# Four segments for five in the choice among equal numbers of a top-p row, and one scan for a scan and a subtraction

## The chip, the cores and the metric

The kernel runs on one core of one Trainium2 chip. The metric is the device time of one execution in microseconds (us). Its engines work side by side, each through its own queue in order: TensorE (PE; PEld is its weight load), VectorE (DVE), ScalarE (ACT), GpSimd (POOL), and SyncE (SP), which here only issues DMAs. They wait for one another through semaphores.

## The reference, cut to what matters

Two graph layers over 2,708 nodes with 256 features. The first multiplies a sparse weighted adjacency matrix by the features, projects the result, adds the input and normalizes. The second runs two steps, each with an attention of top-p kind over all nodes; the change lies in the second of these.

```python
def _top_p_attention(X, W1, W2, W3):
    q = X @ W1.T @ W2.T
    k = X @ W3.T
    probs = jax.nn.softmax(q @ k.T / TAU, axis=-1)
    idx = jnp.argsort(-probs, axis=-1)
    sp = jnp.take_along_axis(probs, idx, axis=-1)
    cs = jnp.cumsum(sp, axis=-1)
    keep_sorted = cs - sp < TOP_P
    mask = jnp.zeros(probs.shape, dtype=bool).at[rows, idx].set(keep_sorted)
    A = probs * mask
    return A / jnp.maximum(A.sum(-1, keepdims=True), 1e-12)
...
for n in range(STEPS):
    A = _top_p_attention(Xa, W1, W2, W3)
    Xf = R @ Xf
    Xa = A @ Xa
    Z = Z + Xf @ U1[n].T + Xa @ U2[n].T
h = X + Z
...
```

In words: of each row, the largest probabilities are kept until their sum reaches 0.9. The number at which that happens is the threshold of the row. Several entries may equal it exactly, and then only the first few of them, in the order of the columns, are kept.

## The kernel before

The rows are cut into 22 blocks of 128 (the last has 20). `fast_path` holds everything that runs on ordinary data; if any of a set of flags is raised on the way, `general_path` computes the second layer anew at the end, which takes far longer.

Stages in time: the adjacency product of layer 0 (to about 290 us), step 1 of the attention (to about 760), step 2 (766 to 1323), a short end with the last normalizations (to 1343.5). No planner orders the work: the order of each engine's queue is the order in which the Python code emits the instructions.

Step 2 is the loop `for per in range(NB + 1)` at L1127. One turn, a period, works on four blocks at once. ACT and PE prepare the exponentials of block `per + 2` (`logits`, `exps2`). ACT tries two levels of the search on block `per + 1` (`try_act`, L921 and L924). DVE finishes block `per` (`last_level`, then `finish2`). PE turns the finished block `per - 1` (L525), ACT copies the turned pieces out of PSUM (L528), and PE multiplies them (L562). The product with R runs beside it in units (`r_units`, L729), fed by gathers that POOL issues (L697). From period 13 on the final normalizations join (`final_slot`, L1036 on DVE, L1046 on ACT, L1061 and L1062 on POOL). Each period has six slots `g`. `finish2` is a generator: it gives up its turn at each `yield`, and the next slot resumes it. In slot 4 it goes from the first sums (L988) through the first three replacements of L1006; after the `yield` there, DVE takes what ends a unit of R (L752, or L767 with a row block of `za` that a DMA has brought), and slot 5 resumes with the rest.

A row is held in 2,720 columns: 2,708 and 12 of padding. What `finish2` does with a block:

- L975: of all entries, take those below an upper level into `w`, and sum them.
- L978: the eight largest of each of 20 pieces of 136 columns, so 160 candidates (`cand`).
- `put_in_order` (L575, L577): the 48 largest of the candidates, in order.
- L988 to L993: running sums, the threshold `th`, and `nk`, how many entries equal to it are to be kept.
- L997: a 1 at each candidate that equals the threshold. L998: how many of them lie in each of `WS` = 5 segments of the row (544 columns each, 32 candidates), in `num`.
- L999: the running sum of these numbers. L1000: number + `nk` - running sum, which is how many equal entries are left to keep at the start of each segment (`run`).
- L1001, L1003: for each segment eight numbers, the threshold as often as entries are to be kept there, else 0 (`part`).
- L1006: for each segment, a copy of the exponentials into `w` in which the first entries equal to the numbers of `part` are replaced by a huge number. Each is two instructions, a load of the eight numbers and the pass over the segment.
- L1009: keep what is above the threshold, and sum it; this releases PE's turning of the block.

A segment that holds eight or more equal entries raises a flag at the end (L1204, L1205).

Of the kernel before, what the change touches and what calls it, by code (L numbers as in the profile page):

```python
# [12 lines left out]
ALU = mybir.AluOpType  # L13
AX = mybir.AxisListType
# [11 lines left out]
NS2 = 20  # L26
TOP1 = 64
TOP2 = 48
WS = 5

# [20 lines left out]
def gnn_two_layer_kernel(ctx: ExitStack, tc: tile.TileContext, N, xT_d, x_d, adj_d, w0_d, b0_d,  # L53
# [71 lines left out]
    with fast:  # L125
        fast_path(fast, tc, c, flags, fint, xT_d, x_d, w0_d, b0_d, w1_d, w2_d, w3_d, u1_d, u2_d, g_d, b_d)
# [22 lines left out]
def fast_path(ctx, tc, c, flags, fint, xT_d, x_d, w0_d, b0_d, w1_d, w2_d, w3_d, u1_d, u2_d, g_d, b_d):  # L149
    nc = tc.nc  # L150
    N, D, DA, NB, DC, KH, CHS, rows = c.N, c.D, c.DA, c.NB, c.DC, c.KH, c.CHS, c.rows
# [234 lines left out]
    for t in range(NB):  # L386
        p = rows(t)
# [57 lines left out]
    for m in range(NB):  # L445
        p = rows(m)
# [123 lines left out]
    def put_in_order(dst, n, cand, p):  # L570

        spare = small.tile([P, NS2 * 8], FP, tag="spare", name="spare", bufs=1)[:, :cand.shape[1]]
        src = cand
        for i in range(0, n, 8):
            nc.vector.max(dst[:p, i:i + 8], src[:p])  # L575
            if i + 8 < n:
                nc.vector.match_replace(spare[:p], dst[:p, i:i + 8], src[:p], -3.0e38)  # L577
                src = spare
# [36 lines left out]
    def finish1(t):  # L615
# [4 lines left out]
        s = srt[:p, :TOP1]  # L620
        sc = small.tile([P, 3 + 2 * WS], FP, tag="sc", name="sc", bufs=3)
        top, mass, tot, fm = (sc[:p, i:i + 1] for i in range(4))
# [158 lines left out]
    def e2(t):  # L781
        return es[(t + 2) % 4]
# [11 lines left out]

    bulk = small.tile([P, 5 + WS, NB], FP, tag="bulk", name="bulk", bufs=1)
    nc.gpsimd.memset(bulk[:, :4, :], 1.0)
# [116 lines left out]
    w = tile1[:, :NW]  # L913
# [52 lines left out]
    def finish2(b):  # L966

        t, p = b.t, b.p
        sc = small.tile([P, 3 + 2 * WS], FP, tag="sc", name="sc", bufs=3)
        num, run = bulk[:p, 5:, t], sc[:p, :WS]  # L970
        need, below, mass, tot = (bulk[:p, i, t:t + 1] for i in range(1, 5))
        nk = sc[:p, WS:WS + 1]
        th = b.m
        e = e2(t)[:p]
        nc.vector.scalar_tensor_tensor(w[:p], e, b.d, e, op0=ALU.is_lt, op1=ALU.mult, accum_out=below)  # L975
        cand = small.tile([P, NS2 * 8], FP, tag="cand", name="cand", bufs=2)
        for i in range(NS2):
            nc.vector.max(cand[:p, 8 * i:8 * i + 8], w[:p, SEG2 * i:SEG2 * (i + 1)])  # L978
            if i in (2, NS2 // 2 + 1):
                yield  # L980
        yield
        srt = small.tile([P, TOP1 + 1], FP, tag="srt", name="srt", bufs=3)
        s = srt[:p, :TOP2]
        put_in_order(srt, TOP2, cand, p)
        yield
        x = sums
        q_ = small.tile([P, TOP1], FP, tag="qs", name="qs", bufs=1)[:p, :TOP2]
        nc.vector.scalar_tensor_tensor(need, b.z, TOP_P - 1.0, below, op0=ALU.mult, op1=ALU.add)  # L988
        nc.vector.tensor_tensor_scan(x[:p, 1:TOP2 + 1], s, s, 0.0, op0=ALU.add, op1=ALU.bypass)
        nc.vector.scalar_tensor_tensor(q_, x[:p, 1:TOP2 + 1], need, s, op0=ALU.is_ge, op1=ALU.mult)  # L990
        nc.vector.tensor_reduce(th, q_, AX.X, ALU.max)
        nc.vector.scalar_tensor_tensor(q_, x[:p, :TOP2], need, s, op0=ALU.is_lt, op1=ALU.mult, accum_out=mass)
        nc.vector.tensor_scalar(q_, q_, th, None, op0=ALU.is_equal, op1=ALU.add, accum_out=nk)  # L993

        eq = small.tile([P, NS2 * 8], FP, tag="spare", name="eq", bufs=1)
        part = small.tile([P, WS, 8], FP, tag="part", name="part", bufs=1)
        nc.vector.tensor_scalar(eq[:p], cand[:p], th, None, op0=ALU.is_equal)  # L997
        nc.vector.tensor_reduce(num, eq[:p].rearrange("p (s k) -> p s k", s=WS), AX.X, ALU.add)  # L998
        nc.vector.tensor_tensor_scan(run, num, num, 0.0, op0=ALU.add, op1=ALU.bypass)  # L999
        nc.vector.scalar_tensor_tensor(run, num, nk, run, op0=ALU.add, op1=ALU.subtract)  # L1000
        nc.vector.tensor_tensor(part[:p], run[:, :, None].to_broadcast([p, WS, 8]),  # L1001
                                ranks[:p, None, :].to_broadcast([p, WS, 8]), op=ALU.is_gt)
        nc.vector.tensor_scalar(part[:p], part[:p], th, None, op0=ALU.mult)  # L1003
        W = NW // WS
        for i in range(WS):
            nc.vector.match_replace(w[:p, W * i:W * (i + 1)], part[:p, i, :], e[:, W * i:W * (i + 1)], 3.0e38)  # L1006
            if i == WS // 2:
                yield
        nc.vector.scalar_tensor_tensor(e, w[:p], th, e, op0=ALU.is_gt, op1=ALU.mult, accum_out=tot)  # L1009
        ra = small.tile([P, 1], FP, tag="ra", name="ra")  # L1010
        nc.vector.reciprocal(ra[:p], tot)
        ras[t] = ra
# [114 lines left out]
    for per in range(NB + 1):  # L1127
# [12 lines left out]
        for g in range(NG):  # L1140
# [28 lines left out]
            if g == 0:  # L1169
                if b_dve:  # L1170
                    last_level(b_dve)
                    masks = finish2(b_dve)
                    next(masks)
                final_slot(0)
                if per > 1:

                    t = t_mul - 1
                    base = za_load(t)
                    later[0].append(lambda t=t, base=base: arrive(t, base, accs.pop(t), ras.pop(t)[:rows(t)]))
            elif masks:  # L1180
                next(masks, None)
                if b_exp and g == 5:
                    begin_search(b_exp)
# [4 lines left out]
    t = EDGE  # L1188
# [3 lines left out]
    for f in later[0] + later[1]:  # L1192
# [8 lines left out]
    nc.vector.tensor_tensor(kept, kept, bulk[:, 0, :], op=ALU.add)  # L1201
    nc.vector.scalar_tensor_tensor(flags[:, 4 * NB:5 * NB], kept, 1.0 + TIE_EPS, bulk[:, 4, :],
                                   op0=ALU.mult, op1=ALU.is_lt)
    nc.vector.tensor_reduce(flags[:, 5 * NB:6 * NB], bulk[:, 5:, :].rearrange("p w t -> p t w"), AX.X, ALU.max)  # L1204
    nc.vector.tensor_scalar(flags[:, 5 * NB:6 * NB], flags[:, 5 * NB:6 * NB], 8.0, None, op0=ALU.is_ge)  # L1205
    nc.vector.tensor_reduce(fcol, flags, AX.X, ALU.add)
    pf = ps_misc()
    nc.tensor.matmul(pf[:1, :1], lhsT=fcol, rhs=onec, start=True, stop=True)
# [386 lines left out]
```

## Time and profile before

| what | value |
|---|---|
| three timed runs | 1348.48, 1345.78 and 1349.26 us; median 1348.48 |
| profiled execution | 1345.32 us, of which 1343.5 are the span of the trace |
| busy over the span | PE 1246.7 us (93%), DVE 1045.5 (78%), ACT 753.4 (56%), POOL 640.1 (48%) |
| chain that ended last, by engine | PE 54%, DVE 38%, ACT 4% |
| its largest lines of DVE | L978 6%, L1006 5%, L1009 5%, L975 4% |
| L978, 128x136, 440 instructions | 284 ns each, 93.5 us |
| L1006, the passes over 128x544, 105 instructions | 709 ns each, 73.5 us |
| mean granted TensorE clock | 0.971 of full speed |

The span is what the trace covers; the profiled execution's own time adds 1.8 us around it. The chain follows the end of the work back, at each step to what released it, or to the instruction before it on its engine. Timelines give start, duration, engine, line, operation, output and inputs with their shapes; "x2" counts instructions that were put together, and a bracket names what ended an idle time.

### The profile page before, as it was taken

Reading aid. Unit: us, or ns where it says so; the run is one execution under the profiler, and the core shown is the slowest. Engines: PE = TensorE matmul, PEld = TensorE weight load, DVE = VectorE, ACT = ScalarE, POOL = GpSimd, SP = SyncE. Lnnn points to the kernel's source line nnn. Section 1 sums busy time; section 2 is a strip of 40 time slices with the busy share of each in tenths; the row PEclk is TensorE's granted clock in tenths of the full one; section 3 lists DMA queues with packets and bytes.
Section 4 is the critical chain, followed back from the end, with each engine's and each line's share of the span. In section 5 each row is a group of like instructions: output and inputs, shape, how many; then the busy total and the mean of one; then the engine's idle time right before and its main releaser. Section 6 shows DMA issues by size and latency. Waiting matters only on the chain.

```text
span 1343.5 us, 18721 instructions
## 1 busy us (share of the span) xinstructions
PE 1246.7 (93%) x5676; PEld 881.0 (66%) x5676; DVE 1045.5 (78%) x3488; ACT 753.4 (56%) x1366; POOL 640.1 (48%) x591
## 2 busy tenths in 40 slices
PE   8999999989899999999999789999998998999885
PEld 6877878833467666667666367676765765666663
DVE  2544545865998888777751599999999999999997
ACT  1010001035556556655555567887878888999851
POOL 1000000004465522777654478877725757777770
PEclk9999999989899999999999889999998999999988
DMA  7455554512131210232223355554522633454341
GB/s 188 163 172 162 164 164 143 166 51 72 60 98 57 71 58 9 74 102 81 71 68 97 98 166 169 148 160 147 161 66 92 191 119 122 150 172 146 122 144 37
DMA packets 92829, 157.92 MB, mean 118 GB/s; under 512 B 16356, under 2 KB 65196, under 8 KB 92720
## 3 DMA queue, kind: packets, MB, share of 16 engines
q1 hardware_dynamic: 66434, 100.59, 23.6%
q0 software_dynamic: 20544, 51.17, 13.4%
q10 hardware_dynamic: 5742, 4.89, 1.3%
q8 instruction: 47, 0.77, 0.2%
q14 instruction: 62, 0.51, 0.1%
HBM read 125.33 MB, written 31.26 MB: 117 GB/s over the span
## 4 chain that ended last, share of the span: by engine, by line
PE 54%; DVE 38%; ACT 4%; issue 2%; POOL 1%; DMA 1%; SPq 0%; ACTq 0%; DVEq 0%; POOLq 0%
PE acc L562 16%; PE acc L255 15%; PE lg L505 6%; DVE cand L978 6%; DVE w L1006 5%; DVE e L1009 5%; DVE w L975 4%; PE tr L525 4%; DVE srt L575 3%; DVE spare L577 3%; PE misc L676 3%; PE acc L648 2%; PE acc L460 2%; PE misc L424 2%; PE misc L390 2%
## 5 line engine op out<-in xcount | busy, mean ns | idle before, releaser
L528 ACT COPY wT<-tr 128x512 f32<-128x512 f32 (+2 forms) x258 | 131.9, 519 | 223.4 <-PE tr L525 219.0
L562 PE MATMUL acc<-ya,wT 128*128 128x256 f32 (+1 forms) x924 | 236.3, 396 | 12.1 <-ACT wT L528 11.7
L697 POOL DMA_INDIRECT yg<-yf_d,ix x154 | 194.8, 1265 | 78.7 <-PE misc L729 40.6
L697 POOL DMA_INDIRECT yg<-v_d,ix x154 | 193.8, 1259 | 79.4 <-DMA v_d<-v 34.0
L562 PE MATMUL acc<-x,wT 128*128 128x256 f32 (+1 forms) x924 | 230.5, 388 | 0.0
L562 PEld LDWEIGHTS acc<-x,wT 128*128 128x128 f32 (+1 forms) x924 | 165.2, 189 | 79.6 <-issue 46.9
L562 PEld LDWEIGHTS acc<-ya,wT 128*128 128x128 f32 (+1 forms) x924 | 172.1, 194 | 68.2 <-ACT wT L528 23.1
L255 PE MATMUL acc<-y,adj_t 128*128 128x257 f32 (+1 forms) x924 | 208.4, 381 | 0.0
L255 PEld LDWEIGHTS acc<-y,adj_t 128*128 128x128 f32 (+1 forms) x924 | 171.8, 189 | 32.7 <-issue 8.9
L365 POOL DMA_INDIRECT adj_t<-in_adj,ix x154 | 164.7, 1069 | 51.5 <-issue 39.9
L729 PE MATMUL misc<-yg,adj_t 128*128 128x256 f32 (+1 forms) x660 | 173.9, 397 | 9.4 <-DVE v L752 9.4
L505 PE MATMUL lg<-k,q 64*128 64x512 f32 (+3 forms) x528 | 150.7, 598 | 21.5 <-ACT e L821 19.5
L525 PE MATMUL tr<-ident,e 128*128 128x128 f32 (+2 forms) x946 | 149.9, 278 | 18.0 <-DVE e L1009 17.9
L729 PEld LDWEIGHTS misc<-yg,adj_t 128*128 128x128 f32 (+1 forms) x660 | 118.4, 193 | 56.1 <-issue 16.2
L525 PEld LDWEIGHTS tr<-ident,e 128*128 128x128 f32 (+2 forms) x946 | 114.0, 141 | 62.2 <-issue 23.9
L332 POOL DMA_DIRECT2D part_d<-e x1 | 0.6, 576 | 286.9 <-DVE e L331 286.9
L568 DVE MAX8 cand<-e 128x8 f32<-128x170 f32 (+1 forms) x352 | 87.3, 318 | 35.4 <-ACT e L512 35.4
L921 ACT ACTIVATE w<-e,st 128x2708 f32<-128x2708 f32 (+1 forms) x43 | 113.5, 2640 | 0.0
L437 ACT COPY x1T<-tr 128x256 f32<-128x256 f32 (+1 forms) x22 | 8.0, 364 | 186.6 <-PE tr L436 186.6
L924 ACT ACTIVATE w<-e,st 128x2708 f32<-128x2708 f32 (+1 forms) x42 | 110.9, 2641 | 0.1
L978 DVE MAX8 cand<-w 128x8 f32<-128x136 f32 (+1 forms) x440 | 93.5, 284 | 0.8
L575 DVE MAX8 srt<-spare 128x8 f32<-128x128 f32 (+3 forms) x264 | 81.3, 308 | 9.1
(228 smaller groups left out, 1761.8 us busy)
## 6 DMA issues: line engine op xcount, KB each, us to landing
adj_t<-in_adj SPq DMA_DIRECT2D x44, 704.0 KB
adj_t<-adjc_d SPq DMA_DIRECT2D x44, 448.0 KB
adjc_d<-adj_t SPq DMA_DIRECT2D x22, 256.0 KB
base<-za_d SPq DMA_DIRECT2D x41, 128.0 KB
adjc_d<-adj_t SPq DMA_DIRECT2D x22, 192.0 KB
xt<-in_x ACTq DMA_DIRECT2D x21, 128.0 KB
x_d<-x SPq DMA_DIRECT2D x21, 128.0 KB
x1b_d<-xb SPq DMA_DIRECT2D x21, 128.0 KB
```

The source lines that it names most:

```text
L255: nc.tensor.matmul(acc[:p, :n], lhsT=halves[k // KH][:kw, k % KH, :p], rhs=y[:kw, k, :n], start=k == 0, stop=stop and k == NB - 1)
L365: nc.gpsimd.indirect_dma_start(out=a[:CW, i, :], out_offset=None, in_=adj_rows, in_offset=bass.IndirectOffsetOnAxis(ap=ix[:CW, m, i:i + 1] ...
L505: nc.tensor.matmul(lg[:p, h, :b - a], lhsT=q[o, t * P:t * P + p], rhs=keys[s][o, i, :b - a], start=True, stop=True)
L525: nc.tensor.transpose(tr[:kw, k % 4, :p], e[:p, k * P:k * P + kw], ident[:p, :p])
L528: nc.scalar.copy(wT[:, :full, :p], tr[:, :full, :p])
L562: nc.tensor.matmul(acc[:p, :D], lhsT=wT[:kw, k % 4, :p], rhs=y[:kw, k, :], start=k == 0, stop=k == NB - 1)
L575: nc.vector.max(dst[:p, i:i + 8], src[:p])
L697: nc.gpsimd.indirect_dma_start(out=y[:CW, i, :], out_offset=None, in_=rows_d, in_offset=bass.IndirectOffsetOnAxis(ap=ix[:CW, m, i:i + 1], ...
L729: nc.tensor.matmul(acc[:p, :D], lhsT=a[:kw, k, :p], rhs=rhs, start=k == 0, stop=k == CC)
L921: nc.scalar.activation(scr[:b.p, :N], e, AF.Relu, bias=b.nz, scale=b.l[k], accum_out=b.relu)
L924: nc.scalar.activation(scr[:b.p, :N], e, AF.Sign, bias=b.nz, scale=b.l[k], accum_out=b.sign)
L978: nc.vector.max(cand[:p, 8 * i:8 * i + 8], w[:p, SEG2 * i:SEG2 * (i + 1)])
```

## The change

The candidates equal to the threshold are counted in four segments of 680 columns (40 candidates each) in place of five of 544. The counts are taken with a minus sign, by the reduction itself. `nk` is written into the first column of `run`, and one running sum, which starts from it and adds the negative counts of the first three segments, fills the other three: `run` holds the same numbers as before, and the addition and subtraction of L1000 is gone. `part` has 32 columns for 40, and L1006 runs four times on 680 columns. The `yield` inside that loop comes after its third turn, as before; behind it stands one turn for two. The flag compares the least of the negative counts with -8; a segment is now wider, and the bound of eight stays.

```diff
-WS = 5
+WS = 4
...
         num, run = bulk[:p, 5:, t], sc[:p, :WS]
         need, below, mass, tot = (bulk[:p, i, t:t + 1] for i in range(1, 5))
-        nk = sc[:p, WS:WS + 1]
+        nk = run[:, 0:1]
...
         nc.vector.tensor_scalar(eq[:p], cand[:p], th, None, op0=ALU.is_equal)
-        nc.vector.tensor_reduce(num, eq[:p].rearrange("p (s k) -> p s k", s=WS), AX.X, ALU.add)
-        nc.vector.tensor_tensor_scan(run, num, num, 0.0, op0=ALU.add, op1=ALU.bypass)
-        nc.vector.scalar_tensor_tensor(run, num, nk, run, op0=ALU.add, op1=ALU.subtract)
+        nc.vector.tensor_reduce(num, eq[:p].rearrange("p (s k) -> p s k", s=WS), AX.X, ALU.add, negate=True)
+        nc.vector.tensor_tensor_scan(run[:, 1:], num[:, :WS - 1], num[:, :WS - 1], nk, op0=ALU.add, op1=ALU.bypass)
...
-    nc.vector.tensor_reduce(flags[:, 5 * NB:6 * NB], bulk[:, 5:, :].rearrange("p w t -> p t w"), AX.X, ALU.max)
-    nc.vector.tensor_scalar(flags[:, 5 * NB:6 * NB], flags[:, 5 * NB:6 * NB], 8.0, None, op0=ALU.is_ge)
+    nc.vector.tensor_reduce(flags[:, 5 * NB:6 * NB], bulk[:, 5:, :].rearrange("p w t -> p t w"), AX.X, ALU.min)
+    nc.vector.tensor_scalar(flags[:, 5 * NB:6 * NB], flags[:, 5 * NB:6 * NB], -8.0, None, op0=ALU.is_le)
```

## The prediction

> **What bounds the kernel now.** I read the page first, then the chain of waits, a table of busy time by stretch of step 2, the waits by engine, and last the timelines of one period on VectorE (DVE) and TensorE (PE). The 40 slices of the page:
>
> ```profile
> PE   8999999989899999999999789999998998999885
> DVE  2544545865998888777751599999999999999997
> PEclk9999999989899999999999889999998999999988
> ```
>
> The change lies in `finish2`, which runs once for each of the 22 row blocks of step 2, from 766 us on. From there DVE stands at 9, with PE at 8 to 9 beside it, so the share of busy time does not settle which of them sets the pace. The chain of waits does, for one block:
>
> ```profile
> 936.73 3.07 DVE w L975 x2
> 940.25 2.09 DVE cand L978 x10
> 952.05 2.17 DVE w L1006 x4
> 956.04 3.07 DVE e L1009 x2
> 961.17 3.07 DVE w L975 x2
> ```
>
> From the L975 of one block to that of the next it never leaves DVE; the period is 961.17 - 936.73 = 24.44 us. DVE reports no wait of any size in these periods; its idle part is the 20 to 40 ns between neighbours. Two periods, before and after the final normalizations join:
>
> ```profile
> core 0: us, PE busy (x) PEld busy (x) DVE busy (x) ACT busy (x) POOL busy (x), PEclk, DMA share, GB/s
> 936.70:961.20 24.50, 23.24 (x113) 17.13 (x112) 23.46 (x80) 19.99 (x34) 18.52 (x15) 1.00 0.50 151
> 1138.00:1165.00 27.00, 24.14 (x113) 17.12 (x112) 25.82 (x90) 25.09 (x41) 21.46 (x19) 1.00 0.47 147
> ```
>
> ```profile
> 957.27 1.03 PE L729 MATMUL misc<-yg,adj_t 128*128 128x256 f32 x4
> 959.25 0.63 PE L525 MATMUL tr<-ident,e 128*128 128x128 f32 x4 [0.94 <-DVE e L1009]
> 1161.76 1.03 PE L729 MATMUL misc<-yg,adj_t 128*128 128x256 f32 x4
> 1162.71 0.63 PE L525 MATMUL tr<-ident,e 128*128 128x128 f32 x4
> ```
>
> In the first period PE stands idle for 0.94 us until L1009 has written the masked block: PE has that much room. In the second the transposes start 0.15 us after DVE's last write for L1009 (1162.56), the same lag as at 959.25, so DVE still paces; but the four matmuls before, which elsewhere let the next start 0.86 us after their first, would have freed PE at 1162.62. The loop of ACT and PE has 0.09 us of room there, in six periods (14 to 19 of 0 to 21; 1111 to 1272 us).
>
> **What the skill says.** "Vector Engine (DVE) Microarchitecture Reference", 5.2 "Measured stream behaviour on trn2": 1.0417 ns for a column and about 75 ns for an instruction after overlap. The trace agrees in the slope: the match-replace takes 276 ns on 128 columns and 709 on 544, that is 1.041 each. "DVE: opcode table, instruction layouts, handler registers and perf-mode slots", 6 "Datapath and trigger behaviour": the scan runs at half rate. It agrees: 170 ns for 5 columns (L999), 256 for 48 (L989), 2.0 each. "SBUF — State Buffer", section "SBUF: two separate sides": DVE and GpSimd share a port pair under an exclusive lock. Here L1003 takes 0.24 us in 17 blocks and 0.47 to 0.49 in 5, and those five begin 0.47 us after the start of a gather on POOL and end where it ends. No page gives the price of a [P, 1] scalar operand.
>
> **The change part by part.** The lines of DVE at stake, of one block (start, duration):
>
> ```profile
> 950.72 0.32 DVE L998 TENSOR_REDUCE bulk<-eq 128x5 f32<-128x160 f32 x1
> 951.07 0.17 DVE L999 TENSOR_TENSOR_SCAN sc<-bulk 128x5 f32<-128x5 f32 x1
> 951.28 0.23 DVE L1000 SCALAR_TENSOR_TENSOR sc<-bulk,sc 128x5 f32<-128x5 f32 x1
> 951.54 0.20 DVE L1001 TENSOR_TENSOR part<-sc,ranks 128x40 f32<-128x40 f32 x1
> 951.77 0.24 DVE L1003 TENSOR_SCALAR part<-part,st 128x40 f32<-128x40 f32 x1
> 952.05 0.09 DVE L1006 MATCH_VALUE_LOAD w<-part,e 128x8 f32 x1
> 952.13 0.71 DVE L1006 MATCH_REPLACE8 w<-part,e 128x544 f32<-128x544 f32 x1
> 952.76 0.08 DVE L1006 MATCH_VALUE_LOAD w<-part,e 128x8 f32 x1
> ```
>
> What counts on a full engine is the distance between starts, not the duration.
>
> 1. L999 and L1000 become one scan over 3 columns. Removed: 951.54 - 951.07 = 0.47 us. Added: L999's 170 ns less two columns at 2.0 (166), plus a start value read from a tile. The trace has no scan with such a start. Nearest rows: a tensor_scalar on one column takes 134 ns with constants (L827), 214 with one tile scalar (L942), 273 with two (L828), so 60 to 80 ns for each. I take 65: 231 ns, and with the usual 33 ns to the next start 0.265. Saved 0.205; ends 0.27 (the read is free) and 0.15 (it costs double). A loss is excluded: the scan would have to take 270 ns more than L999.
> 2. L1006 goes from five pairs over 544 columns to four over 680: the same 2,720 columns, one pair fewer. A pair lies 0.695 us from the next, of which 544 x 1.041 = 0.566 are columns, so 0.129 fixed, and that is saved. Ends 0.11 and 0.15 (the start distances of the pairs scatter from 0.69 to 0.71).
> 3. L1001 and L1003 shrink from 40 columns to 32: 8 ns each at most, 0.015 together. L998 reads the same 160 columns; its negation I cost at nothing, at most 11 ns (L592 with it 181 ns, L594 without 170, same shape).
> 4. The reduce of the flags at the end reads 88 columns for 110: 0.02 us once. One memset on POOL (L797) shrinks far ahead of its use. No DMA is added, removed or moved past another, and PE, ACT, POOL and SP keep their instructions in the same order.
> 5. Moved: the first half of L1006, ahead of the yield, still has three pairs, now 3 x 0.142 = 0.43 us longer. The L752 or L767 behind it therefore starts about 0.2 us later in its block, net of points 1 and 3. It frees a PSUM bank and lets a row of `v` or `za` be stored; the bank that L767 frees at 1158.1 is written next at 1161.8. More than 3 us of room, no cost. What follows it, one pair for two, is shorter by more.
>
> Sum for a block: 0.205 + 0.129 + 0.015 = 0.35 us (ends 0.27 and 0.43). Times 22: 7.7 us (5.9 to 9.4).
>
> **Whether it reaches the end.** In periods 0 to 13, PE's 0.94 us shrinks to some 0.6 and every 0.35 counts (in the two of them in which PE shows no wait, from 790 and from 1034 us, it makes up for it in the next). In the six tight periods ACT and PE can follow by 0.09 only; DVE gains 0.26 on them each time, 1.6 us in all. It is not stopped at once, since it does not wait for the loop at the period's start: the nearest thing it needs is a `za` row from DMA landing 2.0 us before its use (1182.69 against 1184.68), then `yg` from POOL with 3.0 (1175.15 against 1178.18), then L958 after ACT's last small step with about 4. In period 20 the exponentials are gone and PE waits 3.4 us for L1009, room for the 1.6. After the last block the chain is mostly DVE again (1322 to 1337 us), so all 22 savings arrive.
>
> Against the profiled execution, 1345.32 us (span 1343.5): 1345.32 - 7.7 = 1337.6. That execution was the fastest of four, 3.2 us below the median of the three timed ones (1348.48); their common mean is 1347.2, so I forecast 1347.2 - 7.7 = 1339.5, or -0.57%.
>
> **Rivals.**
>
> A. The loop of ACT and PE holds: DVE meets a wait once it is ahead, and in the six tight periods only 0.09 comes through. 16 x 0.35 + 6 x 0.09 = 6.1 us, 1341.1. For it: the room of 0.09. Against: the 2 to 4 us that DVE may run ahead.
>
> B. Port holds eat the gain. A small tensor_scalar that begins 0.45 to 0.85 us into a gather waits up to 0.25 us for its end. L1003 moves up by 0.2 us in its block, which at the present phases releases the five held ones (-1.2 us) and catches three others by 0.08 us each; but the gathers, 1.25 us apart, move too. If most blocks were caught at both L997 and L1003, 0.2 to 0.25 us each, the gain would fall to between 0 and 4 us: about 1345. For it: six holds are there already. Against: 16 of 22 blocks have none, and nothing aims at that window.
>
> C. Slower: PE's clock. The granted clock is 0.93 in 790 to 815 us, where PE is busy all of its 24.3 us. A denser step could draw such a grant in periods 1 to 9: (23.14 / 0.94) + 0.3 of waits = 24.9 against 24.44 now, +0.45 x 9 = 4.1; in the six tight periods about 4 us of the loop are PE, +0.25 against the 0.09, so +0.16 x 6 = 1.0; the other seven keep -0.35, -2.4. Together +2.7 us, 1350. It decides below a grant of 23.14 / (24.44 - 0.3) = 0.96. Against: most periods show 1.00 with PE at 95%.
>
> That the change makes more flags is a rival in kind: a segment may now hold the equals of 680 columns before the slow general path is entered at 8. Numbers exactly equal to a threshold are rare in a row of float exponentials; 1%, and far slower.
>
> **Chances.** Forecast 0.65, A 0.12, B 0.15, C and the flags 0.08. About 0.3%, 4.0 us, is what a measurement here tells from no change. The forecast and A are faster by more (0.77), B is within (0.15), C and the flags slower (0.08). Range: low 1347.2 - 9.4 - 2 of scatter = 1335.5; high from the upper half of B, 1345.5. What is left out is the slow side and the rest of B.
>
> **What would show it.** Right: L975 to L975 at 24.1 us before 1050; a scan of about 0.23 us; L1006 of 0.85 us four times a block; PE's wait for L1009 near 0.6 in the first periods and none in the tight ones. Wrong: a DVE wait at L767 or L1036 after 1110 (A), tensor_scalars of 0.4 to 0.5 us in most blocks (B), a granted clock below 0.96 over many periods (C), a scan above 0.4 us.

## The result, and the profile after

The changed kernel takes 1338.76 us in the median of four runs (1337.47 to 1339.33), before it was 1348.7: a ratio of 0.9929, with a 95% interval from 0.9912 to 0.9947. Run once more, the pair gave 0.9934 (0.9920 to 0.9948). The profiled execution took 1338.91 us, its span 1337.1.

The 40 slices of the page after, to be laid beside those of before:

```profile
PE   8999999979899999999999979999998998899885
DVE  2445555865998888877761399999999999999997
PEclk9999999989899999999999779999999989999987
```

They look the same, as they must: DVE is as full as before and only comes through its work sooner. The chain of waits for one block shows it (start, duration):

```profile
935.45 3.07 DVE w L975 x2
...
950.62 2.60 DVE w L1005 x5
953.22 0.39 DVE v L752
953.61 0.85 DVE w L1005
954.49 3.07 DVE e L1008 x2
...
959.61 3.05 DVE w L975
```

From L975 to L975 it is 959.61 - 935.45 = 24.16 us, where it was 24.44, and the chain still never leaves DVE. The operations at stake, from DVE's timeline of the same block:

```profile
949.45 0.32 DVE L998 TENSOR_REDUCE bulk<-eq 128x4 f32<-128x160 f32 x1
949.81 0.22 DVE L999 TENSOR_TENSOR_SCAN sc<-bulk,sc 128x3 f32<-128x3 f32 x1
950.07 0.19 DVE L1000 TENSOR_TENSOR part<-sc,ranks 128x32 f32<-128x32 f32 x1
950.29 0.29 DVE L1002 TENSOR_SCALAR part<-part,st 128x32 f32<-128x32 f32 x1
950.62 0.09 DVE L1005 MATCH_VALUE_LOAD w<-part,e 128x8 f32 x1
950.70 0.85 DVE L1005 MATCH_REPLACE8 w<-part,e 128x680 f32<-128x680 f32 x1
951.47 0.08 DVE L1005 MATCH_VALUE_LOAD w<-part,e 128x8 f32 x1
```

The scan and what follows it lie 0.26 us apart, where scan and subtraction took 0.47. L1002, with fewer columns than before, is longer (0.29 against 0.24); this comes back below. PE and the end of L1008, from their timelines:

```profile
956.00 1.03 PE L729 MATMUL misc<-yg,adj_t 128*128 128x256 f32 x4
957.69 0.63 PE L525 MATMUL tr<-ident,e 128*128 128x128 f32 x4 [0.66 <-DVE e L1008]
...
1237.60 1.03 PE L729 MATMUL misc<-yg,adj_t 128*128 128x256 f32 x4
1238.47 0.60 PE L525 MATMUL tr<-ident,e 128*128 128x128 f32 x4
...
1290.37 0.63 PE L525 MATMUL tr<-ident,e 128*128 128x128 f32 x4 [2.89 <-DVE e L1008]
```

```profile
1237.25 0.08 DVE L1008 DVE_READ_ACCUMULATOR e<-w,st,e 128x1 f32 x1
```

PE's room in the early period has shrunk from 0.94 to 0.66 us. In the tight period DVE is done with the block at 1237.33, and PE takes it up only at 1238.47, as soon as its four matmuls have gone in: DVE is ahead by 1.14 us. At 1290.37 PE waits for DVE again.

A single number carries the comparison of traces from here on: the distance from the first L975 to the last, 21 periods. It repeats within 0.04 us for one kernel (524.03 and 524.07 in two traces of after), while what lies around it scatters: step 2 began between 764.3 and 767.4 us in the traces, with the same code ahead of it, and the part behind the last L975 took 44.6 to 46.9. Before was traced once, in an execution of 1345.32 us; its 531.76 us have no second reading.

| kernel | distance in step 2, us | against before | median, us | ratio to before (95%) |
|---|---|---|---|---|
| before | 531.76 | | 1347.2 to 1348.7 | |
| after | 524.03 | -7.73 | 1338.76 | 0.9929 (0.9912 to 0.9947) |
| after, once more | 524.07 | -7.69 | 1338.74 | 0.9934 (0.9920 to 0.9948) |
| scan alone, five segments | 526.58 | -5.18 | 1340.46 | 0.9942 (0.9929 to 0.9955) |
| four segments alone | 527.70 | -4.06 | 1341.78 | 0.9956 (0.9943 to 0.9969) |
| after, yield behind the last pass | 521.98 | -9.78 | 1336.62 | 0.9916 (0.9902 to 0.9929) |
| after, L1002 as a product | 522.82 | -8.94 | 1335.30 | 0.9920 (0.9906 to 0.9933) |
| two segments, flag at nine | 515.51 | -16.25 | 1330.22 | 0.9874 (0.9859 to 0.9889) |
| two segments, nine, product | 514.22 | -17.54 | 1328.89 | 0.9869 (0.9853 to 0.9884) |
| one segment, no bound | 509.35 | -22.41 | 1321.40 | 0.9807 (0.9794 to 0.9820) |

### The profile page after: what moved, and what is told of

It is laid out like the page before. It is cut to its first block, busy times and chain, and to the rows that moved or that the text cites. A ratio compares the mean times of both kernels' runs of the same rounds, so it can differ in the third digit from the quotient of the medians.

```text
span 1337.1 us, 18655 instructions
## 1 busy us (share of the span) xinstructions
PE 1247.3 (93%) x5676; PEld 881.5 (66%) x5676; DVE 1038.0 (78%) x3422; ACT 752.9 (56%) x1366; POOL 645.6 (48%) x591
## 4 chain that ended last, share of the span: by engine, by line
PE 53%; DVE 39%; ACT 3%; DMA 2%; issue 2%; SPq 0%; ACTq 0%; DVEq 0%
PE acc L562 16%; PE acc L255 15%; PE lg L505 6%; DVE cand L978 6%; DVE w L1005 6%; DVE e L1008 5%; DVE w L975 5%; PE tr L525 4%; PE misc L676 3%; DVE srt L575 3%; DVE spare L577 3%; PE acc L648 2%; PE acc L460 2%; PE misc L424 2%; DMA base<-za_d 1%
## 5 line engine op out<-in xcount | busy, mean ns | idle before, releaser
L697 POOL DMA_INDIRECT yg<-yf_d,ix x154 | 199.2, 1293 | 72.5 <-PE misc L729 35.7
L562 PEld LDWEIGHTS acc<-x,wT 128*128 128x128 f32 (+1 forms) x924 | 165.2, 189 | 79.5 <-issue 46.9
L978 DVE MAX8 cand<-w 128x8 f32<-128x136 f32 (+1 forms) x440 | 93.5, 284 | 0.8
```

Source lines behind the costliest of these rows:

```text
L562: nc.tensor.matmul(acc[:p, :D], lhsT=wT[:kw, k % 4, :p], rhs=y[:kw, k, :], start=k == 0, stop=k == NB - 1)
L697: nc.gpsimd.indirect_dma_start(out=y[:CW, i, :], out_offset=None, in_=rows_d, in_offset=bass.IndirectOffsetOnAxis(ap=ix[:CW, m, i:i + 1], ...
```

## The experiments

**The two parts, each alone.** The first keeps the scan that starts from `nk` and goes back to five segments; the second is the kernel before with four.

```diff
 (after)
-WS = 4
+WS = 5
```

> The changed kernel with five segments of 544 columns again: only the scan that starts from the number to keep is left of the change. Theory (VectorE sets the period and each part of the change counts by its distance between starts): the scan and the subtraction of before lay 0.47 us apart from the next operation, the one scan of after 0.26, so 0.21 us a block: periods of 24.23 us from L975 to L975 before the final normalizations join (24.44 before, 24.14 after), 4.6 us less than before over 22 blocks, about 1344. Rival (the gain is in the passes over the row, the scan's start value costs what the subtraction did): periods of 24.4 us and no change of time.

```diff
 (before)
-WS = 5
+WS = 4
```

> The kernel before with four segments of 680 columns: only the count of segments is changed, the scan and the subtraction stay. Theory: one fixed cost of a load and pass less, 0.129 us, and 0.015 us from shorter small operations: periods of 24.30 us, 3.2 us less than before, about 1345.5; together with the run of the scan alone the whole gain of the change. Rival (the yield that now comes behind 2,040 columns, with a late L752 and L767, costs something): periods above 24.30 us.

The scan alone gave early periods of 24.23 and 24.24 us in five blocks and 24.29 or 24.30 in three, four segments alone 24.29 or 24.30. Each part is worth what its start distances say, and both rivals are out: the scan does pay, and the later L752 costs nothing. The sum over step 2 is larger than expected in both, 5.18 for 4.4 and 4.06 for 3.0 us (21 periods). The small tensor_scalar accounts for this (L1003, L1002 in the kernels with the new scan): before, it took 0.47 to 0.49 us in five blocks, 1.2 us more than 22 times 0.24; with the scan alone it did so in none and with four segments in one, and its sum over the blocks fell by 0.85 and 1.06 us. Counted once, the two parts make 5.18 + 4.06 - 1.2 = 8.0 us; together in after they gave 7.73.

**Two segments, to have more of the same.**

```diff
 (after)
-WS = 4
+WS = 2
```

> The changed kernel with two segments of 1,360 columns; both passes now lie ahead of the yield. Theory: two fixed costs less (0.26 us) and 0.04 us from shorter small operations: periods of 23.84 us where after has 24.14; in the six tight periods VectorE at 26.15 us runs ahead of the loop of ScalarE and TensorE (26.65 us) by 0.5 each, 3 us in all, and the transposes that wait for L1008 start later and later behind it, until period 20 gives it back. 6.6 us less than after, about 1332. Rival (VectorE cannot be 3 us ahead: it meets a wait for a row from DMA or from GpSimd): waits on VectorE after 1110 us, periods of 26.65 us among the tight ones, and 1 to 2 us less of the gain, 1333 to 1334.5.

The time was 6539.59 us. The first lines of its page:

```profile
span 6537.6 us, 37665 instructions
...
PE   9999899880432244123303323322421430432331
DVE  4687699949999999999999988999999999999998
```

Nearly five times the span and twice the instructions, with DVE full to the end: the flag was raised and `general_path` ran. Step 2 itself lies ahead of the flag, and its trace shows 515.37 us from the first L975 to the last, 8.7 less than after where 6.6 were expected, periods of 23.73 to 23.77 (23.84 expected) and then 25.99 to 26.07 us (26.15 expected), and no wait on DVE. So the theory held on the course of step 2 and the rival fell, but the kernel as it stood was of no use. Why the flag: in a recomputation of the reference, 712 of the 2,708 rows of step 1 keep one entry only, so that many rows of `Xa` are copies of one another and many columns of step 2 hold exactly the same number. The most entries equal to the threshold in one segment, by the same recomputation, are 5 with 544 columns, 6 with 680, 8 with 1,360 (in 71 rows) and 13 in a whole row. The next run tests the eight.

```diff
 (two segments)
-    nc.vector.tensor_scalar(flags[:, 5 * NB:6 * NB], flags[:, 5 * NB:6 * NB], -8.0, None, op0=ALU.is_le)
+    nc.vector.tensor_scalar(flags[:, 5 * NB:6 * NB], flags[:, 5 * NB:6 * NB], -9.0, None, op0=ALU.is_le)
```

> Two segments of 1,360 columns as in the run before, and the flag raised at nine equal entries in a segment, no longer at eight. Theory (the run with two segments left the fast path because some row has exactly eight equal entries in one segment, which the eight numbers of a pass can still hold): no general path, and the step-2 distance of that run's trace, 515.4 us from the first L975 to the last against 524.0 of after, so 8.7 us less than after, about 1330. Rival (rows with more than eight): the general path again, about 6,540 us.

1330.22 us and 515.51 in step 2: the fast path again, so in no segment were nine counted. The count sees eight candidates of each piece of 136 columns (L978), so a piece with nine equal entries counts as eight at most: a bound of eight takes a full count as a sign, a bound of nine cannot see it. On this input the recomputation finds at most three in a piece.

**One segment.** No running sum; the count comes with the comparison, and one operation makes the eight numbers.

```diff
 (after)
-WS = 4
+WS = 1
...
-        nc.vector.tensor_scalar(eq[:p], cand[:p], th, None, op0=ALU.is_equal)
-        nc.vector.tensor_reduce(num, eq[:p].rearrange("p (s k) -> p s k", s=WS), AX.X, ALU.add, negate=True)
...
+        nc.vector.tensor_scalar(eq[:p], cand[:p], th, None, op0=ALU.is_equal, op1=ALU.add, accum_out=num)
+        nc.vector.tensor_scalar(part[:p, 0, :], ranks[:p], nk, th, op0=ALU.is_lt, op1=ALU.mult)
```

> One segment of 2,720 columns: no running sum at all; the count comes with the comparison of L997, and one operation makes the eight numbers. Theory: VectorE saves 1.2 us a block against after and is no longer what bounds: TensorE had 0.64 us of room in the first periods, so these go to 23.5 us; in the tight ones the loop of ScalarE and TensorE stays at 26.65; VectorE waits. The sum for TensorE: 13 x 0.64, then nothing in six periods, then the waits of 2.9 and 1.6 us for the last two blocks: 12.8 us less than after, about 1326. Rival (VectorE alone sets the time): periods of 22.95 us and 26 us less, 1313.

6529.87 us, by the same flag (thirteen equal entries). Step 2 took 509.33 us, 14.7 less than after where 12.8 were expected. With the bound raised to 1,000:

> One segment with the bound on equal entries left out (raised to 1,000): a row with more than eight entries to keep at its threshold keeps eight. Theory (TensorE bounds the first periods, the loop of ScalarE and TensorE the tight ones, VectorE waits once it is 5.2 us ahead): the step-2 distance of the trace with one segment, 509.3 us against 524.0 of after, 14.7 us less, 1324 to 1326. Rival (VectorE alone): 26 us less than after, 1313.

509.35 us in step 2, as expected, and 1321.40 us in the median, 2.6 below the lower end of what was expected; the rival's 26 us are far off. The periods tell where the rest of DVE's saving stayed: 22.75 us in periods 2 to 4, 23.3 in periods 6 to 9, 26.64 and 26.65 in four of the tight ones. In periods 6 to 9 PE is busy for 23.0 us and waits 0.31 for ACT, never for DVE; the loop of ACT and PE in the tight ones takes 26.65. DVE's waits in step 2 (total, times, longest), and two of them from its timeline:

```profile
DVE st L958 <- ACT st L937: 6.9, 11, 1.3
DVE nmax L814 <- PE lg L505: 2.4, 8, 0.4
DVE bst L1031 <- POOL yg L1057: 2.0, 6, 0.8
```

```profile
1141.68 0.29 DVE L814 TENSOR_REDUCE nmax<-lg 128x1 f32<-128x128 f32 x1 [0.29 <-PE lg L505]
1142.69 0.22 DVE L958 SCALAR_TENSOR_TENSOR st<-st 128x1 f32<-128x1 f32 x1 [0.71 <-ACT st L937]
```

(L1031 here is L1035 of after, L1057 its L1061.) No row from DMA is among them. The issue of the last `za` row of a period and the L767 of that period:

```profile
1187.69 0.43 SPq L746 DMA_DIRECT2D base<-za_d  x1
1190.48 0.47 DVE L767 SCALAR_TENSOR_TENSOR h<-misc,rinv,base 128x256 f32<-128x256 f32 x1
```

The packets of that row ran on until 1192.48, 2 us after L767 had started without a wait: L767 reads one of the rows loaded before.

How far DVE was ahead, as the start of PE's transposes behind the end of L1008, in us, for blocks 13 to 20:

| kernel | 13 | 14 | 15 | 16 | 17 | 18 | 19 | 20 |
|---|---|---|---|---|---|---|---|---|
| before | 0.15 | 0.15 | 0.15 | 0.14 | 0.15 | 0.15 | 0.15 | 0.15 |
| after | 0.14 | 0.36 | 0.56 | 0.77 | 0.98 | 1.14 | 1.12 | 0.15 |
| two segments, nine | 0.14 | 0.82 | 1.46 | 2.10 | 2.75 | 3.39 | 4.00 | 0.15 |
| one segment, no bound | 4.87 | 5.25 | 5.23 | 5.24 | 5.23 | 5.25 | 5.22 | 0.15 |

0.15 is the plain lag of a release. Rows two and three climb by the difference of the two loops, 26.65 less DVE's period, and fall back in period 20. The last row stands at 5.2: that is how far DVE can be ahead, and from there each period is the loop's.

**The yield behind the last pass.** The two segments had saved 0.38 us a block where the parts made 0.30. With two segments both passes lie ahead of the yield, and L752 or L767 behind them.

```diff
 (after)
-            if i == WS // 2:
+            if i == WS - 1:
```

> The changed kernel with the yield behind the fourth pass of L1005 in place of the third, nothing else. Theory (the two-segment run saved 0.08 us a block more than the sum of its parts, because L752 or L767 then lies between the last pass and L1008, and L1008 no longer starts right behind the pass that writes what it reads): 0.12 us less a block, periods of 24.02 us, 2.6 us less than after in all. Rival (the order of these two does not matter, and the 0.08 us has another cause): periods of 24.14 us as in after; or more, if the unit of R that frees its bank 0.8 us later holds TensorE.

Early periods of 24.00 to 24.03 us; 2.05 us less in step 2, for 2.6 expected. From its timeline, and then from that of after:

```profile
951.97 0.85 DVE L1005 MATCH_REPLACE8 w<-part,e 128x680 f32<-128x680 f32 x1
952.74 0.47 DVE L752 SCALAR_TENSOR_TENSOR v<-misc,rinv,v 128x256 f32<-128x256 f32 x1
953.13 3.04 DVE L1008 SCALAR_TENSOR_TENSOR e<-w,st,e 128x2720 f32<-128x2720 f32 x1
```

```profile
953.60 0.85 DVE L1005 MATCH_REPLACE8 w<-part,e 128x680 f32<-128x680 f32 x1
954.49 3.05 DVE L1008 SCALAR_TENSOR_TENSOR e<-w,st,e 128x2720 f32<-128x2720 f32 x1
```

Behind a pass whose result it reads, L1008 starts 0.89 us after the pass's start; L752, which does not read it, 0.77 after, and L1008 then 0.39 after L752. The rival is out. L1008 so starts 0.04 us after the end of that pass, and L752 0.08 before the end of its own. That the reading makes the difference fits small operations in the timeline of after:

```profile
958.42 0.21 DVE L958 SCALAR_TENSOR_TENSOR st<-st 128x1 f32<-128x1 f32 x1
958.54 0.15 DVE L959 SCALAR_TENSOR_TENSOR st<-st 128x1 f32<-128x1 f32 x1
958.66 0.21 DVE L960 TENSOR_SCALAR st<-st 128x1 f32<-128x1 f32 x1
958.91 0.22 DVE L961 SCALAR_TENSOR_TENSOR st<-st 128x1 f32<-128x1 f32 x1
```

L959 reads nothing of L958 and starts 0.07 to 0.09 us before the end of L958; L961 reads what L960 writes and starts 0.035 us after its end; both in all 22 blocks.

The gain fades in the late tight periods, which take 26.43 to 26.61 us where the earlier ones take 26.33 to 26.36. There L997, itself a tensor_scalar, took 0.37, 0.54 and 0.54 us in blocks 17 to 19 for its usual 0.30, and ended each time 0.06 to 0.07 us after a gather.

**L1002 as a product of two tiles.**

```diff
 (after)
-        nc.vector.tensor_scalar(part[:p], part[:p], th, None, op0=ALU.mult)
+        nc.vector.tensor_tensor(part[:p], part[:p], th[:, :, None].to_broadcast([p, WS, 8]), op=ALU.mult)
```

> The changed kernel with L1002 as a product of two tiles (the threshold spread over the 32 columns) in place of a tensor_scalar; nothing else. Theory (L1002 is held by a gather of POOL, as its ends at the gathers' ends suggest, and a product of two tiles is not held, as L1000 is not): it takes 0.19 us as L1000 does and the next starts 0.23 after it, 0.10 us earlier where L1002 was held (0.33) and 0.04 earlier where it was not (0.27): periods of 24.04 us where after has 24.14, and 1.5 us less than after in step 2. Rival (what follows L1000 waits for its result, whatever it is): the product too ends where a gather ends, and the periods stay at 24.14 us.

L1002 by kernel (least, median, greatest ns): first after, then this run.

```profile
L1002 DVE TENSOR_SCALAR part<-part,st x22: 228/268/317, 782.3 to 1308.5; 128x32 f32<-128x32 f32 x21, 20x32 f32<-20x32 f32 x1
```

```profile
L1002 DVE TENSOR_TENSOR part<-part,st x22: 178/192/194, 779.3 to 1304.3; 128x32 f32<-128x32 f32 x21, 20x32 f32<-20x32 f32 x1
```

The spread is gone and the early periods are 24.05 and 24.06 us; 1.2 us less in step 2 (1.5 expected). In after, L1002 was 0.29 to 0.32 us long in eleven blocks, and in ten of them it ended with a gather of POOL. For the one at 950.29, which ended at 950.58, this is the gather:

```profile
949.64 0.95 POOL L697 DMA_INDIRECT yg<-yf_d,ix  x1 [0.30 <-PE misc L729]
```

The product began 0.63 to 0.67 us into a gather in eleven blocks, where a tensor_scalar had been held, and took 0.19 us in each. So it was the gather, and not the wait for L1000, that held L1002.

**Both together with two segments.** The product of the run above in the kernel with two segments and the flag at nine, the shortest that keeps a bound at all:

> Two segments with the flag at nine, and L1002 as a product of two tiles: what the runs so far suggest as the shortest that keeps the flags. Theory: the two savings add, 515.5 - 1.5 = 514 us from the first L975 to the last, 1.5 us less than with two segments alone, 1329. Rival (TensorE has no room left in the first periods, where its own period is 23.3 us): no gain over two segments, 1330.

514.22 us in step 2, 1.3 less, and 1328.89 in the median, with a ratio to before of 0.9869 (0.9853 to 0.9884). Its interval overlaps that of two segments alone, so the step from the one to the other rests on the distance in the trace. Against after it is some 10 us.

**After once more**, beside the runs with two segments, one segment and the yield:

> The changed kernel once more, on the same chip as the three others. Theory: 524 us from the first L975 to the last, and 7.7 to 10 us less than before, 1338 to 1341. If the part of the first result beyond 7.7 us lay outside step 2, the step-2 distance repeats within 0.5 us and the rest scatters.

524.07 us in step 2 and 1338.74 in the median. After's distance is fixed; before's rests on one trace. What a pair of medians shows beyond the 7.7 us (8.6 here, 9.9 in the first result) would then lie outside step 2, where single traces differ by 2 to 3 us. Chance alone it may not be: every changed kernel of the table gained more in the median than in step 2, by 0.8 to 3.5 us. The trace of before is of an execution 2 to 3 us faster than its medians, so a longer step 2 in the others is not excluded; this stays open.

## Why the prediction was right, and where it was not

- *The number.* 1339.5 us were forecast and 1338.76 measured; 7.7 less were forecast, the medians gave 9.9 and step 2 in the traces 7.73. That the last agrees so closely is luck in part, as part 3 shows.
- *What bounds.* Right. Every edit of DVE's work in `finish2` moved step 2 by its start distances, until one segment put PE and the loop of ACT and PE in its place.
- *Part 1, the scan.* 231 ns expected, 223 measured; 0.205 saved, 0.21 measured.
- *Part 2, one pass fewer.* 0.129 expected; the start distances of all passes of a block sum to 3.47 us for 3.60 before, 0.13 saved.
- *Part 3, the smaller operations.* Mis-sized: 0.015 saved was expected, but L1002 came 0.2 us earlier against the gathers and was held for 0.05 to 0.08 us in eleven blocks (three in the text on rival B). An early period fell by 0.28 to 0.30 us for 0.35. The five long holds of before were gone, as that text had counted (1.2 us), but the sum had left them out. Holds of L1002 took 0.66 us back and one more hold of L997 0.15, so 0.4 us came on top of 21 x 0.35 = 7.35 us: 7.73. The forecast had its 7.7 from 22 blocks, the last of which lies outside this distance, so it is luck that the two numbers meet.
- *Part 5, the move.* Right that it costs nothing. It left 0.12 us a block lying there: the order of L752 and the last pass has a price that was not seen.
- *Whether it reaches the end.* Right in its course: PE's room 0.66 us for some 0.6, the loop of ACT and PE 26.65 for 26.68, DVE ahead by 1.0 beyond the plain lag for 1.6 (0.2 gained in each of five periods, not 0.26 in six), all given back in period 20. Rival A fell.
- *How far DVE may run ahead.* This step was wrong. The nearest wait was put at 2.0 us, a row of `za` from DMA. With two segments DVE was 4.0 us ahead and waited for nothing; with one segment it stopped at 5.2, at ACT's last small step (L958), which had been put at about 4, at PE's logits (L814) and at POOL's `yg`, which had been put at 3.0. No row from DMA was among its waits. The prediction had timed the wrong row: its 1182.69 is the landing of the last of three rows loaded in a period, and with one segment L767 started before that one had come (run of one segment). Why `yg` held DVE later than 3.0 us is not shown. It did no harm here, since 1.1 us were needed.
- *Equal numbers are rare.* Wrong in its reason. They are common on this input; four segments stay below the bound by two (6 of 8, by the recomputation), and the flag was not raised, but its chance was set on a false ground. Two segments reached it (8 of 8).
- *Rival C.* The mean granted clock was 0.970 in the trace after and 0.971 before, and 1.00 in both from 814 to 1006 us, where the denser step was feared.

## What to carry to other kernels

On an engine that is full, take the distance between starts from a timeline and multiply by the count; here that was good to 0.01 us for each part. Holds by another engine are not in it: they moved the sums by up to 1 us. Beside it, lay out for the second loop how much room it has in a period and how far the first can run ahead of it: a saving beyond the room is not lost if a later stretch gives the time back. And before a bound on ties is taken to be idle, count the ties in the data: the rows that a sparse step copies are equal to the last bit. And ask what the counter can see before the bound is moved.

## What the runs showed of the hardware that was not expected

- A pass that is followed at once by an operation reading its result costs 0.12 us more than one followed by another (0.89 against 0.77 us between starts). Small operations show the same: 0.035 us after the end of the one before, against 0.07 to 0.09 before its end.
- A small tensor_scalar is held until a gather on POOL ends if it begins in that gather's later part: held at 0.47 to 0.52 us after the gather's start for 0.2 to 0.25 us, at 0.63 to 0.66 for 0.05 to 0.08, and not at 0.46 or less. A product of two tiles in its place took 0.178 to 0.194 us in all 22 blocks.
- The scan's start value from a tile costs 60 ns: for 4 columns it takes 227 ns in the run of the scan alone, and 167 with a constant in the run of four segments. The prediction had taken 65.
